# Two slot tiles of expert 0 inside the last tiles' routing of a GNN-plus-mixture-of-experts kernel

## The chip, the cores and the metric

The kernel runs on one core of one Trainium2 chip. The metric is the device time of an execution in microseconds (us). Before the change it is 1527.41 us, the median of three runs (1524.62 to 1529.33). One further execution was taken by the hardware profiler: its own time is 1522.34 us, of which 1520.5 us is the span from the first to the last instruction of the core. Durations below come from that execution. The engines are called PE (TensorE, matrix products; PEld is its weight load), DVE (VectorE), ACT (ScalarE), POOL (GpSimd) and SP (SyncE, which here only issues transfers).

## What is computed

1250 rows of 768 numbers pass a two-layer graph attention network and then one transformer block whose feed-forward part is a mixture of eight experts. The change touches only the end:

```python
x = x + _attention(_layernorm(x, ln1_g, ln1_b), Wqkv, Wproj)
x = x + _moe(_layernorm(x, ln2_g, ln2_b), Wrouter, W1, W2)
...
logits = xf @ Wrouter                          # 8 experts
topk_w, topk_idx = jax.lax.top_k(logits, 2)
topk_w = softmax(topk_w)
...
h = gelu(xf @ W1e)                             # 768 -> 384
acc = acc + we_e[:, None] * (h @ W2e)          # 384 -> 768
```

Only the two chosen experts of a token have a weight other than zero, so the kernel computes each expert for its own tokens alone.

## The kernel before

**Stages.** Ahead of the change stand the graph layers and the attention. Then comes a projection and routing stage over ten tiles of 125 tokens (`NT`, `T`), and last an expert stage. The two are the subject here.

**Projection and routing.** `product(t)` (L860) multiplies the attention's result with the projection weights (L864), adds the residual, takes the second layer norm into `yn` (one of three buffers of `RW` = 772 columns) and writes the sum `xs` to `out` (L875; even tiles are written from SP's queue, odd ones from ACT's). `route(t)` (L878) transposes `yn` (helper, L141), lets ACT apply the norm's scale and bias into `fT` (L147), forms the logits `pl` (L883), and DVE finds the best two experts. A product with a triangular matrix (`prk`, L900) and one with the tokens seen so far (L902, `seen`) give each token its rank within its expert. Rank plus 1280 times the expert is the slot. Columns 768 to 771 of `yn` take the token's number, its first expert and the two softmax weights; these use an Exp on ACT (L911). Two indirect transfers from POOL's queue (L923) then scatter the 125 rows into the DRAM buffer `xd`, one for each chosen expert. In the loop at L936 tile t+1's product is written ahead of tile t's route, and a scheduler interleaves them. `first_w`, the weights of expert 0, is loaded early in this stage (L854).

**Tiles beyond.** Every expert has three slot tiles of 128 rows (`CAP` = 384). After the last route, L943 to L951 count the slot tiles beyond that: one such tile (`EXTRA`) has a fixed job of its own, and any more are worked off by the conditional loop at L1032, whose number of passes (`more`) each engine loads into a register (L1031).

**Experts.** A job is an expert's three slot tiles, or the one extra tile. `fetch` (L967) loads slot rows from `xd` by SP (L970). `turn` (L991) transposes them on PE (L996) and lets ACT scale them (L997). `first` (L1001) is the first product with Gelu: 36 records on PE for each job (L1006). `second` (L1011) makes, for each slot tile, 12 records of the second product (L1015); DVE adds the weighted result to the row gathered from `out` (L1019; `results`, L986, is the gather on POOL), and POOL scatters it back (L1020). While job i runs its second product, job i+1's weights (L841, L842) and then its rows are loaded, and its rows are transposed between the second product's records. Loads, fetches and the register loads of `place` (L821, L822) all stand on SP's queue.

**What sets the order.** Tiles of a pool have a fixed number of buffers, and a transfer waits until the buffer it takes is free. Waits are set from what reads or writes the same tile or DRAM buffer; scatters into `xd` are declared independent of each other. The fetches of expert 0's rows (L1024) come after all scatters, and the conditional loop stands between that fetch and the first `turn` (L1046).

Of the kernel before, what the change touches and what calls it, by code (L numbers as in the profile page):

```python
# [10 lines left out]
F32 = mybir.dt.float32  # L11
F16 = mybir.dt.float16
BF16 = mybir.dt.bfloat16
I32 = mybir.dt.int32
# [13 lines left out]
def gnn_ffn_kernel(  # L28
# [27 lines left out]
    P = 128  # L56
# [22 lines left out]
    RW = D + 4  # L79
# [767 lines left out]

    with tc.tile_pool(name="proj", bufs=3, reuse_waits="tile") as pp, \
            tc.tile_pool(name="ppo", bufs=2, space=PSUM) as ppo, \
# [5 lines left out]

        normed = [pp.tile([P, RW], F32, tag=f"yn{i}", name=f"yn{i}", bufs=1) for i in range(3)]
# [3 lines left out]
        def product(t):  # L860
            po = ppo.tile([T, 2, 512], F32, tag="po", name="po")
            for s in range(2):
                for c in range(DC):
                    nc.tensor.matmul(po[:, s, :DH], aT[:, c, t * T:(t + 1) * T],  # L864
                                     wp[:, c, s * DH:(s + 1) * DH],
                                     start=(c == 0), stop=(c == DC - 1))
            y2 = pp.tile([T, D], F32, tag="y2", name="y2")
            ln_apply(y2, xs[:, t, :], st0[:, 0, t:t + 1], st0[:, 1, t:t + 1])
            o = y2.rearrange("p (s d) -> p s d", s=2)
            nc.vector.tensor_tensor(o, o, po[:, :, :DH], ALU.add)  # L870
            mean, rstd = ln_stats(y2)
            yn = normed[t % len(normed)]
            ln_apply(yn[:T, :D], y2, mean, rstd)
            nc.vector.tensor_add(xs[:, t, :], xs[:, t, :], y2)
            split_rows(nc.sync if t % 2 == 0 else nc.scalar, out[t * T:(t + 1) * T, :], xs[:, t, :])  # L875
            return yn

        def route(t, yn, seen):  # L878
            fT = pp.tile([P, DC, T], F32, tag="fT", name="fT", bufs=2)
            transpose_rows(ppt, yn[:T, :D], affine(fT, 0, 2))  # L880
            pl = ppl.tile([P, 512], F32, tag="pl", name="pl")
            for c in range(DC):
                nc.tensor.matmul(pl[:T, :NE], fT[:, c, :], wr[:, c, :],  # L883
                                 start=(c == 0), stop=(c == DC - 1))
            lg = small.tile([T, NE], F32, tag="lg", name="lg")
# [12 lines left out]
            nc.vector.tensor_add(both, oh[:, 0, :], oh[:, 1, :])  # L898
            pr = ppl.tile([P, 512], F32, tag="pl", name="prk")
# [8 lines left out]

            ex = small.tile([T, 2], F32, tag="ex", name="ex")
            nc.vector.tensor_sub(ex[:, 0:1], top[:, 1:2], top[:, 0:1])  # L910
            nc.scalar.activation(ex[:, 0:1], ex[:, 0:1], AF.Exp)  # L911
            nc.vector.tensor_scalar(ex[:, 1:2], ex[:, 0:1], 1.0, None, ALU.add)
            nc.vector.tensor_copy(yn[:T, D:D + 1], number[:, t:t + 1])
            nc.vector.tensor_copy(yn[:T, D + 1:D + 2], atf[:, 0:1])
            nc.vector.reciprocal(yn[:T, D + 2:D + 3], ex[:, 1:2])
            nc.vector.tensor_mul(yn[:T, D + 3:D + 4], ex[:, 0:1], yn[:T, D + 2:D + 3])
# [10 lines left out]
            return new  # L927
# [6 lines left out]
        yns = [product(0)]  # L934
        seen = None
        for t in range(NT):  # L936
            if t + 1 < NT:
                yns.append(product(t + 1))
            seen = route(t, yns[t], seen)


        pn = ppl.tile([P, 512], F32, tag="pl", name="pn")
        nc.tensor.matmul(pn[:, :NE], ones, seen, start=True, stop=True)  # L943
        count = small.tile([P, 1], F32, tag="count", name="count")
        nc.vector.scalar_tensor_tensor(used, pn[:, :NE, None].to_broadcast([P, NE, NR]), 0.0, used,
                                       op0=ALU.add, op1=ALU.is_gt, accum_out=count)
        nc.vector.tensor_scalar(more, count[0:1], -float(EXTRA), 0.0, ALU.add, ALU.max)
        nc.vector.tensor_tensor(used, used, beyond, ALU.mult)
        for i in range(EXTRA):
            pick(-1.0e9 if i == 0 else picked[:, i - 1, 1:2], i)  # L950
        nc.vector.tensor_copy(picked[:, EXTRA, :], picked[:, EXTRA - 1, :])  # L951
# [5 lines left out]
    with tc.tile_pool(name="moe", bufs=2, reuse_waits="tile") as mp, \  # L957
# [9 lines left out]
        def fetch(rows, n):  # L967
            xr = mp.tile([P, NS, RW], F32, tag="xr", name="xr")
            for s in range(n):
                nc.sync.dma_start(xr[:, s, :], rows[s * P:(s + 1) * P, :])  # L970
            return xr

        def tokens(xr, e, n, tag):

            ids = mp.tile([P, NS], I32, tag=tag + "ids", name="ids")
            nc.vector.tensor_copy(ids[:, :n], xr[:, :n, D])
            weight = mp.tile([P, NS], F32, tag=tag + "weight", name="weight")
            part = mp.tile([P, NS], F32, tag=tag + "part", name="part")
            nc.vector.tensor_sub(part[:, :n], xr[:, :n, D + 2], xr[:, :n, D + 3])
            nc.vector.scalar_tensor_tensor(part[:, :n], xr[:, :n, D + 1], e, part[:, :n],  # L980
                                           op0=ALU.is_equal, op1=ALU.mult)
            nc.vector.tensor_add(weight[:, :n], part[:, :n], xr[:, :n, D + 3])
            return ids, weight

        def results(ids, s, row):
            nc.gpsimd.indirect_dma_start(  # L986
                out=row, out_offset=None, in_=out,
                in_offset=bass.IndirectOffsetOnAxis(ap=ids[:, s:s + 1], axis=0),
                bounds_check=N - 1, oob_is_err=False)

        def turn(xr, n):  # L991
            xT = mp.tile([P, DC, CAP], F32, tag="xT", name="xT")
            for c in range(DC):
                pt = mpt.tile([P, 512], F32, tag="pt", name="pt")
                for s in range(n):
                    nc.tensor.transpose(pt[:, s * P:(s + 1) * P], xr[:, s, c * P:(c + 1) * P], ident)  # L996
                nc.scalar.activation(xT[:, c, :n * P], pt[:, :n * P], AF.Identity,  # L997
                                     scale=lnp[:, 2, c:c + 1], bias=lnp[:, 3, c:c + 1])
            return xT

        def first(w1, xT, n):  # L1001
            hT = mp.tile([P, FC, CAP], F32, tag="hT", name="hT")
            for f in range(FC):
                ph = mph.tile([P, 512], F32, tag="ph", name="phe")
                for c in range(DC):
                    nc.tensor.matmul(ph[:, :n * P], w1[:, c, f * P:(f + 1) * P], xT[:, c, :n * P],  # L1006
                                     start=(c == 0), stop=(c == DC - 1))
                nc.scalar.activation(hT[:, f, :n * P], ph[:, :n * P], AF.Gelu)
            return hT

        def second(w2, hT, s, ids, weight, row):  # L1011
            po = mpo.tile([P, 2, 512], F32, tag="po", name="poe")
            for d in range(2):
                for f in range(FC):
                    nc.tensor.matmul(po[:, d, :DH], hT[:, f, s * P:(s + 1) * P],  # L1015
                                     w2[:, f, d * DH:(d + 1) * DH],
                                     start=(f == 0), stop=(f == FC - 1))
            o = row.rearrange("p (s d) -> p s d", s=2)
            nc.vector.scalar_tensor_tensor(o, po[:, :, :DH], weight[:, s:s + 1], o, op0=ALU.mult, op1=ALU.add)  # L1019
            nc.gpsimd.indirect_dma_start(  # L1020
                out=out, out_offset=bass.IndirectOffsetOnAxis(ap=ids[:, s:s + 1], axis=0),
                in_=row, in_offset=None, bounds_check=N - 1, oob_is_err=False)

        xr = fetch(xd[0:CAP, :], NS)  # L1024
# [6 lines left out]
        over = nc.values_load(more[0:1, 0:1], min_val=0, max_val=NE * NR)  # L1031
        with tc.For_i(0, over, 1):  # L1032
# [5 lines left out]
            ids, weight = tokens(xo, picked[:, EXTRA, 0:1], 1, "o")  # L1038
            results(ids, 0, sofar[0])
            second(w2, first(w1, turn(xo, 1), 1), 0, ids, weight, sofar[0])  # L1040

        extra = [place(i) for i in range(EXTRA)]
        jobs = [(float(e), NS, expert(e), lambda e=e: xd[e * REG:e * REG + CAP, :]) for e in range(NE)]
        jobs += [(picked[:, i, 0:1], 1, chosen(e), lambda r=r: xd[ds(r, P), :])
                 for i, (e, r) in enumerate(extra)]
        xT = turn(xr, NS)  # L1046
        for i, (e, n, _, _) in enumerate(jobs):
            w1, w2 = w
            hT = first(w1, xT, n)
            ids, weight = tokens(xr, e, n, "")  # L1050
# [3 lines left out]
            if i + 1 < len(jobs):  # L1054
                _, m, ws, slots = jobs[i + 1]
                w = load_expert(mp.tile([P, 2 * DC * FF], F32, tag="w", name="we"), *ws)
                xr = fetch(slots(), m)
                xT = turn(xr, m)
            for s in range(n):
                second(w2, hT, s, ids, weight, rows[s])  # L1060
# [31 lines left out]
```

## Time and profile before

| What | us |
|---|---|
| Median of three runs | 1527.41 |
| Profiled execution, its own time | 1522.34 |
| Its span | 1520.5 |
| PE busy in the span | 1433.7 (94%) |
| DVE / ACT / POOL busy | 811.9 / 595.6 / 418.6 |
| Bytes moved | 124.66 MB, 82 GB/s on average |
| Tile 9's (the last tile's) scatters start on POOL | 1284.71 and 1285.99 |
| First fetch of expert 0's rows is issued | 1291.10 |
| First product of expert 1 starts | 1326.67 |
| Last scatter of results starts | 1513.17 |

The page gives the busy time of each engine, the span in 40 slices, the chain of work that ended last, and groups of instructions with what ended the idle time before them. A product in 32-bit floats appears as two records on PE. The operations of the change's stages in this execution:

| Operation | count, us of one |
|---|---|
| L864 product record, 384 columns | 240; 38 in a row take 12.45 |
| L1006 first-product records of one job, 384 columns | 36 take 11.61 |
| L1006 the same with 128 columns (the extra job) | 36 take 4.18 |
| L1015 second-product records of one slot tile | 12 take 3.87 |
| L997 eviction of transposed rows, 384 / 128 columns | 0.67 / 0.40 |
| L1019 weighted add on DVE | 1.02 |
| L923, L986, L1020 indirect transfer on POOL | 0.98 / 1.03 / 1.00 |
| Table load on ACT | 1.28 |
| `more` read into a register (L1031), by engine | 0.31 to 0.58 |

The granted clock of PE over the whole span is 0.963 of full speed.

### The profile page before, as it was taken

Reading aid. Unit: us, or ns where it says so; the run is one execution under the profiler, and the core shown is the slowest. Engines: PE = TensorE matmul, PEld = TensorE weight load, DVE = VectorE, ACT = ScalarE, POOL = GpSimd, SP = SyncE. Lnnn points to the kernel's source line nnn. Section 1 sums busy time; section 2 is a strip of 40 time slices with the busy share of each in tenths; the row PEclk is TensorE's granted clock in tenths of the full one; section 3 lists DMA queues with packets and bytes.
Section 4 is the critical chain, followed back from the end, with each engine's and each line's share of the span. In section 5 each row is a group of like instructions: output and inputs, shape, how many; then the busy total and the mean of one; then the engine's idle time right before and its main releaser. Section 6 shows DMA issues by size and latency. Waiting matters only on the chain.

```text
span 1520.5 us, 15858 instructions
## 1 busy us (share of the span) xinstructions
PE 1433.7 (94%) x5952; PEld 779.0 (51%) x5952; DVE 811.9 (53%) x1311; ACT 595.6 (39%) x924; POOL 418.6 (28%) x276
## 2 busy tenths in 40 slices
PE   6787999999999999999999999999989996899997
PEld 4574555556555555543343343344333664565654
DVE  6688456434036640127778778778787764111111
ACT  4221513205116521136556646646656354221211
POOL 5000000000000010006646646655657222122222
PEclk9758999999999999999999999999999997899999
DMA  7000020010021139920000000000120432855643
GB/s 207 22 2 11 11 73 0 0 32 1 15 88 45 57 100 396 407 86 0 22 1 0 22 1 21 1 22 0 28 75 1 144 119 107 300 172 185 219 153 134
DMA packets 48199, 124.66 MB, mean 82 GB/s; under 512 B 5629, under 2 KB 22207, under 8 KB 48120
## 3 DMA queue, kind: packets, MB, share of 16 engines
q1 hardware_dynamic: 31468, 57.36, 11.5%
q0 software_dynamic: 11968, 56.26, 9.8%
q10 hardware_dynamic: 4684, 9.99, 2.2%
q8 instruction: 48, 0.79, 0.2%
q14 instruction: 31, 0.25, 0.1%
HBM read 70.47 MB, written 57.60 MB: 84 GB/s over the span
## 4 chain that ended last, share of the span: by engine, by line
PE 67%; DVE 9%; issue 7%; ACT 4%; DMA 4%; POOL 1%; POOLq 0%; SPq 0%; ACTq 0%; DVEq 0%
PE pagg L524 13%; PE st L676 8%; PE ph L204 7%; PE pav L720 7%; PE pk L639 5%; PE pv L655 5%; PE phe L1006 5%; PE poe L1015 5%; PE pq L639 4%; DMA xd<-yn,slot 2%; DVE sT L706 2%; PE po L864 2%; ACT sT L679 1%; DVE most L685 1%; PE mb L701 1%
## 5 line engine op out<-in xcount | busy, mean ns | idle before, releaser
L712 POOL TENSOR_TENSOR acc<-acc,sT 125x834 f32<-125x834 f32 (+1 forms) x139 | 273.1, 1964 | 10.9
L524 PE MATMUL pagg<-h,wt 125*125 125x385 f32 (+1 forms) x800 | 263.5, 486 | 0.4 <-DVE wt L517 0.4
L685 DVE TENSOR_TENSOR most<-most,st 125x834 f32<-125x834 f32 (+1 forms) x144 | 147.0, 1021 | 105.5 <-ACT sT L679 102.6
L524 PEld LDWEIGHTS pagg<-h,wt 125*125 125x125 f32 x800 | 147.0, 187 | 104.7 <-DVE wt L517 3.5
L706 DVE TENSOR_TENSOR sT<-sT,mb 125x834 f32<-125x834 f32 (+1 forms) x180 | 174.1, 1015 | 22.6 <-PE mb L701 22.6
L707 ACT ACTIVATE sT<-sT 125x834 f32<-125x834 f32 (+1 forms) x180 | 158.4, 900 | 49.2 <-DVE sT L706 48.8
L679 ACT COPY sT<-st 125x834 f32<-125x834 f32 (+1 forms) x180 | 151.6, 848 | 52.4 <-PE st L676 50.7
L676 PE MATMUL st<-qk 64*125 64x417 f32 (+1 forms) x720 | 164.5, 556 | 3.9 <-DVE most L685 3.8
L720 PE MATMUL pav<-sT,v 125*64 125x417 f32 (+1 forms) x720 | 151.0, 532 | 9.0 <-ACT sT L707 9.0
L617 POOL MEMSET zero<- 128x772 f32 x1 | 0.7, 742 | 530.2 <-PE ptr L141 530.2
L712 POOL TENSOR_TENSOR acc<-sT 125x834 f32<-125x834 f32 (+1 forms) x18 | 35.4, 1965 | 274.6 <-ACT sT L707 274.6
L676 PEld LDWEIGHTS st<-qk 64*125 64x125 f32 x720 | 56.5, 184 | 99.1 <-issue 42.7
L720 PEld LDWEIGHTS pav<-sT,v 125*64 125x64 f32 x720 | 42.5, 136 | 105.7 <-issue 43.9
L1015 PE MATMUL poe<-we,hT 128*128 128x384 f32 x264 | 88.8, 486 | 0.0
L639 PE MATMUL pq<-yT,wqk 128*128 128x417 f32 (+1 forms) x216 | 88.1, 534 | 0.0
L864 PE MATMUL po<-wp,aT 128*125 128x384 f32 x240 | 87.5, 498 | 0.0
L1019 DVE SCALAR_TENSOR_TENSOR sofar<-poe,weight,sofar 128x768 f32<-128x768 f32 x25 | 25.4, 1018 | 114.6 <-PE poe L1015 107.7
L1006 PE MATMUL phe<-xT,we 128*128 128x384 f32 (+1 forms) x288 | 86.6, 460 | 0.0
L639 PE MATMUL pk<-yT,wqk 128*128 128x417 f32 (+1 forms) x216 | 84.0, 526 | 0.0
L204 PE MATMUL ph<-gw,xnT 128*125 128x384 f32 x240 | 81.4, 498 | 0.5 <-DMA gw<-in_L_gnn_W_dram 0.5
L655 PE MATMUL pv<-wv,yT 128*125 128x384 f32 x240 | 79.9, 490 | 1.4 <-issue 1.4
L528 DVE RECIPROCAL rz<-pagg 125x1 f32<-125x1 f32 x20 | 3.3, 166 | 141.5 <-PE pagg L524 141.5
(222 smaller groups left out, 1788.2 us busy)
## 6 DMA issues: line engine op xcount, KB each, us to landing
xd<-zero POOLq DMA_DIRECT2D x8, 3860.0 KB, 15.2
we<-in_L_ffn_W_dram SPq DMA_DIRECT2D x16, 1152.0 KB
xr<-xd SPq DMA_DIRECT2D x25, 386.0 KB
gw<-in_L_gnn_W_dram SPq DMA_DIRECT2D x2, 2304.0 KB
wqk<-in_L_ffn_Wqkv_dram SPq DMA_DIRECT2D x12, 384.0 KB
xres<-in_x_dram SPq DMA_DIRECT2D x10, 375.0 KB
xsd<-xres ACTq DMA_DIRECT2D x10, 375.0 KB
xn<-in_x_dram SPq DMA_DIRECT2D x9, 336.0 KB
```

The costliest lines, as they stand in the source:

```text
L204: nc.tensor.matmul(po[:, s, :DH], xT[:, c, t * T:(t + 1) * T], w[:, c, s * DH:(s + 1) * DH], start=(c == 0), stop=(c == DC - 1))
L524: nc.tensor.matmul(po[:, s, :DH + s], ws[j][:, (d - d0) * T:(d - d0 + 1) * T], h[:, j, s * DH:(s + 1) * DH + s], start=(j == 0), stop=(j = ...
L639: nc.tensor.matmul(pq[:, :w], wqk[:, c, i, :], yT[:, c, c0:c0 + w], start=(c == 0), stop=(c == DC - 1))
L676: nc.tensor.matmul(st[:T, i, :w], self.qk[r, 1, j * T:(j + 1) * T], self.qk[r, 0, self.c0:self.c0 + w], start=True, stop=True)
L679: nc.scalar.copy(s[:, :, :w], st[:T, :, :w])
L685: nc.vector.tensor_tensor(self.most[:, :, :w], prev[:, :, :w], st[:T, :, :w], ALU.max)
L706: nc.vector.tensor_tensor(s[:, :, :w], s[:, :, :w], self.mb[:T, :, :w], ALU.subtract)
L707: nc.scalar.activation(s[:, :, :w], s[:, :, :w], AF.Exp)
L712: nc.gpsimd.tensor_tensor(self.acc[:, :, :w], prev[:, :, :w], s[:, :, :w], ALU.add)
L720: nc.tensor.matmul(self.pav[r, :w], v[:, j, hd0:hd0 + HD], s[:, i, :w], start=(j == 0), stop=(j == NT - 1))
L1006: nc.tensor.matmul(ph[:, :n * P], w1[:, c, f * P:(f + 1) * P], xT[:, c, :n * P], start=(c == 0), stop=(c == DC - 1))
L1015: nc.tensor.matmul(po[:, d, :DH], hT[:, f, s * P:(s + 1) * P], w2[:, f, d * DH:(d + 1) * DH], start=(f == 0), stop=(f == FC - 1))
```

## The change

Four things are done.

1. **Routing without Exp.** `yn` has 771 columns: token number, first expert, and the difference of the two best logits. The weights are formed in the expert stage, by `tokens`, as 0.5 plus or minus half of tanh(difference / 2), where ACT computes the Tanh (pinned in program order after the Gelu). The token number is now written at the end of `product`.
2. **Two slot tiles of expert 0 within routing.** After tile 6's route, the count of expert 0's tokens is taken; if it is under 256, the running count is lifted so that later tokens get slots from 256 on. The first two slot tiles (256 rows) are then fetched on SP into `xr0`. The last three tiles' steps are written out by hand in PE's order: `go` advances `route` of tiles 7, 8, 9, `product` of tile 9 and `early`, a generator that transposes the two slot tiles, runs their first product with 256 columns, gathers the rows from `out`, and runs both second products with their adds and scatters into `out`. The two gathers stand on POOL ahead of tile 8's and tile 9's scatters.
3. **Tiles beyond counted earlier.** `tiles_beyond` stands ahead of `early`'s last third of the first product and of its second products.
4. **Slot rows ahead of weights.** Expert 0's job keeps its third slot tile only; that fetch is issued on SP ahead of the register load of `more`. In the job loop the next job's rows are fetched before its weights, in program order. The register loads of `place` stand behind the loop on SP, and four of the six `sofar` clears on POOL do too.

The new PE order, the loop and the job loop:

```diff
+        def early(w1, w2):
+            for xT in turn(xr0, SOON, sp, ppt, "tr"):
+                yield None
+            for hT in first(w1, xT, SOON, sp, ppl, "pl"):
+                yield None
+            ids, weight = tokens(xr0, 0.0, SOON, sp, "")
+            for s in range(SOON):
+                results(ids, s, soon[s])
+            for s in range(SOON):
+                second(w2, hT, s, ids, weight, soon[s], ppo)
+                yield None
...
+            if t == WITH - 1:
+                pn = ppl.tile([P, 512], F32, tag="pl", name="pfirst")
+                seen = tally[-1]
+                nc.tensor.matmul(pn[:, :NE], ones, seen, start=True, stop=True)
+                lift = small.tile([1, 1], F32, tag="lift", name="lift")
+                nc.vector.tensor_scalar(lift, pn[0:1, 0:1], -1.0, float(SOON * P), ALU.mult, ALU.add)
+                nc.vector.scalar_tensor_tensor(seen[0:1, 0:1], lift, 0.0, seen[0:1, 0:1], op0=ALU.max, op1=ALU.add)
+                xr0 = sp.tile([P, SOON, RW], F32, name="xr0")
+                for s in range(SOON):
+                    ins = nc.sync.dma_start(xr0[:, s, :], xd[s * P:(s + 1) * P, :])
...
+        with tc.manual_schedule(engines={mybir.EngineType.PE}):
+            a, b = route(NT - 3, yns[NT - 3], tally), product(NT - 1)
+            go(b, 3)
+            go(a)
+            go(b, 2)
+            go(a)
+            go(b, 4)
+            go(a, 2)
+            go(b, 3)
+            yns.append(go(b))
+            x = early(*w)
+            a, b = (route(t, yns[t], tally) for t in (NT - 2, NT - 1))
+            go(a)
+            go(x, DC)
+            go(a)
+            go(b)
+            go(x)
+            go(a, 2)
+            go(b)
+            go(x)
+            go(b, 2)
+            tiles_beyond(tally[-1])
+            go(x)
+            go(x, SOON)
...
-        xr = fetch(xd[0:CAP, :], NS)
+        xr, ins = fetch(xd[SOON * P:CAP, :], NS - SOON, pin)
...
-        over = nc.values_load(more[0:1, 0:1], min_val=0, max_val=NE * NR)
+        with tc.issue_after(ins.ins):
+            over = nc.values_load(more[0:1, 0:1], min_val=0, max_val=NE * NR)
+            extra = [place(i) for i in range(EXTRA)]
...
             if i + 1 < len(jobs):
                 _, m, ws, slots = jobs[i + 1]
+                xr, _ = fetch(slots(), m, pin)
                 w = load_expert(mp.tile([P, 2 * DC * FF], F32, tag="w", name="we"), *ws)
-                xr = fetch(slots(), m)
-                xT = turn(xr, m)
+                xT = last(turn(xr, m, mp, mpt, "pt"))
```

The weights of a slot row in `tokens`:

```diff
-            nc.vector.tensor_sub(part[:, :n], xr[:, :n, D + 2], xr[:, :n, D + 3])
-            nc.vector.scalar_tensor_tensor(part[:, :n], xr[:, :n, D + 1], e, part[:, :n],
-                                           op0=ALU.is_equal, op1=ALU.mult)
-            nc.vector.tensor_add(weight[:, :n], part[:, :n], xr[:, :n, D + 3])
+        pin(nc.scalar.activation(lead, xr[:, :n, D + 2], AF.Tanh, scale=0.5))
+        nc.vector.tensor_scalar(weight, xr[:, :n, D + 1], e, -0.5, ALU.is_equal, ALU.add)
+        nc.vector.tensor_mul(weight, weight, lead)
+        nc.vector.tensor_scalar(weight, weight, 0.5, None, ALU.add)
```

## The prediction

> **What bounds the kernel now.** I read the busy tenths of the page first. TensorE (PE) is at 9 of 10 nearly everywhere; its one late hole lies in slices 34 and 35, where its granted clock falls too.
>
> ```profile
> PE   6787999999999999999999999999989996899997
> ...
> PEclk9758999999999999999999999999999997899999
> ```
>
> The chain of work in order of time (start us, length, what) names the hole. The scatters of routed rows into `xd` end it, then the first fetch of slot rows, and dense products start only at 1302.
>
> ```profile
> 1262.47 27.77 DMA xd<-yn,slot x2
> 1291.10 0.37 SPq L970
> 1291.53 0.42 SPq L970
> 1292.00 5.05 DMA xr<-xd
> ...
> 1302.46 10.32 PE phe L1006 x32
> ...
> 1326.67 11.61 PE phe L1006 x36
> ```
>
> From 1326.67 (expert 1's first product) to the end, PE works without a gap in periods of 25.5 us (1326.67, 1352.18, 1377.68): 11.61 first product, 11.61 second, 2.3 transposes. So I measure the change by the moment at which expert 1's first product starts. The table of stretches (length; busy PE, PEld, DVE, ACT, POOL; granted clock; DMA share; GB/s) shows PE empty, then at half clock, then full:
>
> ```profile
> 1286.00:1291.00 5.00, 0.00 (x0) 0.00 (x0) 0.28 (x3) 0.00 (x0) 0.97 (x1) 0.50 0.42 163
> ...
> 1294.00:1298.00 4.00, 2.06 (x6) 0.87 (x6) 0.57 (x4) 0.40 (x1) 0.43 (x1) 0.50 0.97 313
> 1298.00:1302.00 4.00, 3.67 (x14) 2.57 (x15) 0.00 (x0) 2.32 (x5) 2.69 (x3) 0.62 1.04 399
> 1302.00:1306.00 4.00, 4.00 (x16) 2.54 (x16) 0.00 (x0) 2.87 (x4) 0.00 (x0) 1.00 1.03 408
> ```
>
> Last, the rows of the conditional loop (L1032). No pass of it runs, yet every engine leaves it through a row of waits, which end together at 1290.9 to 1291.5, and SP's list of waits (us in total, times, longest), the second fence, names what came last:
>
> ```profile
> L1032 SPq EVENT_SEMAPHORE  x16: 17/28/28, 1288.3 to 1290.9; - x16
> L1032 PEldq EVENT_SEMAPHORE  x13: 51/51/51, 1285.2 to 1291.4; - x13
> ```
>
> ```profile
> SPq L1032 <- DMA xd<-yn,slot: 1.5, 2, 1.0
> ```
>
> The skipped loop is therefore a barrier: each engine waits there for all work and transfers issued ahead of it. The last scatter starts on POOL at 1285.99, so the barrier costs 5.5 us from the start of the last indirect DMA to PE's release (1291.5). This decides the sum, because the change puts new work ahead of that barrier.
>
> **The change, part by part.** All times stand on before's clock.
>
> *Data.* Worked out from the reference's inputs, the first seven token tiles bring expert 0 269 tokens, which is over 256: the lift is zero and two slot tiles are full in time. Expert 0 has 369 in all (under 384); only expert 6 (419) goes beyond, by one tile. No pass of the loop runs, as before.
>
> *Exp removed from routing.* Two table loads of 1.28 us per tile leave ACT. PE is full there (10.16 us from prk to prk: 24 product records of 0.328 make 7.9, the rest routing), so tiles 0 to 5 gain nothing. But tile 6's scatter no longer waits for the Exp columns: POOL waited 10.93 us for L916 until 1261.18, while its slots were ready at 1256.36. It now starts near 1256.8, the second near 1258.1, and lands near 1262.3 (landings 3.0 to 3.4 us after the descriptors).
>
> *New fetch of two slot tiles* on SP, ahead of tile 8's output write there: issued near 1262.4, as that write becomes ready (1262.78), so it delays nothing. A fetch from issue to use took 3.3 us (1291.10 to 1294.39), the second row 1 us more: 1266.6. VectorE (DVE) waits for it (`ids`) in the middle of tile 7's routing, reaching it near 1266; PE needs that routing at 1267.9. Cover: about 1 us. Beyond that it costs one for one.
>
> *PE up to the early transposes.* From 1255.75: 36 product records x 0.328 = 11.8, two row transposes 1.3, tile 7's logits 1.1, ranks and count 0.8: 1270.8. The same work in before ended at 1270.7, so nothing is gained or lost here.
>
> *Twelve transposes.* They wait on two shared PSUM buffers, so ACT paces them: tile 8's evictions 2.2 (six x 0.365), two of 256 columns (between 0.40 at 128 and 0.67 at 384: 0.53), tile 9's root 0.3 and its two write issues 0.65, then four more. PE is through them at 1276.2. Tile 8's logits and tile 9's transposes stand behind: 1278.0.
>
> *First and second product of the two tiles.* 36 records at 256 columns lie between 4.18 us (128) and 11.61 (384): 7.9. Each third waits for a hand-off: tile 9's logits for the first Gelu (a table load 1.28 ahead of it: 1281.6), the tile-beyond count for the second Gelu, the last third for the rank read. With ranks 0.5 + 0.5, logits 1.1 and count 0.3 this ends at 1289.1; 24 records of the second product at 0.3225 = 7.7: 1296.9. The last routing slots come 2.2 us later than before (1286.6 against 1284.4), but no longer decide.
>
> *The clock, where a rule speaks against.* The Trainium skill, "TensorE: Matmul & The Clock Gate" (Part 1: The HAM clock gate), says that an idle window of about 3.4 us halves the clock and as much sustained work restores it. The row shows a longer stay: 0.50 from 1274 through 1298 over sparse work, full 4 us after dense work began. By the rule alone 3.4 us of the early work run at half speed, 1.7 lost; by the row perhaps all until the second product, 6 lost; by neither, 0. I take 1.7, since pieces of 2.6 us stand close together: second product done at 1298.6. The ends, 1296.9 and 1303, go into the range.
>
> *What then stands ahead of the barrier.* DVE adds the second tile (1.02), POOL starts its scatter 0.3 later, plus 5.5: PE is released 6.9 us after its second product, at 1305.5. Everything behind the barrier waits with it: the slot rows and weights of expert 1, and the remaining tile. The count of tiles beyond and the last slot tile's fetch (scatter landed near 1292.6, fetch 1296) are done by then; this is what the reordered count buys.
>
> *After the barrier.* The last job shows a one-tile job:
>
> ```profile
> 1503.66 4.18 PE L1006 MATMUL phe<-xT,we 128*128 128x128 f32 x36
> ...
> 1507.68 4.04 PE L1015 MATMUL poe<-we,hT 128*128 128x384 f32 x12
> ```
>
> Transposes paced by ACT (six x 0.40, with starts 2.9), then the rest of the first product: 6.0 us after the release. SP meanwhile loads two registers (0.77 and 0.48 with their checks: 1.8 us, now behind the barrier), issues three fetches (1.3) and expert 1's weights. Rows are there 7.3 us after release: PE stalls 1.3. Eighteen transposes of 384-wide rows paced by ACT (six x 0.67) with 12 product records between take 5.9: 13.2; with the clock 0.8: 14.0. Weights of 1.18 MB per half, queued behind 1.2 MB of rows at some 400 GB/s, land near 9 us. Rows ahead of weights thus matter only here, and W1 has 5 us to spare; in the steady 25.5 us periods either order is hidden.
>
> *Per job.* The added Tanh (0.2 as Exp took) stands between Gelu and the next eviction on ACT; PE may see 0.1 of it in seven jobs: 0.7. The removed DVE operations there, and 771 against 772 columns, I put at 0 (bounds -0.5 and +0.5), DVE being busy 4 us in 30.
>
> *Queues moved past.* POOL's two gathers (1.03 each) stand ahead of tile 8's scatters and wait for tile 9's output write, issued near 1274.4. With 3.3 to land they end at 1280.4; the scatters are due at 1281.7. If the write lands 4 us later, they slip into the barrier's slack of 9 us. The cleared `sofar` rows (0.8 each) now follow on POOL, two ahead of the barrier inside the 3.2 us of landing.
>
> *Sum.* Expert 1 starts at 1305.5 + 14.0 = 1319.5 instead of 1326.7: 7.2 gained; less 0.7 per-job cost: 6.5. Span 1520.5 - 6.5 = 1514.0; the profiled execution, 1522.34, becomes 1515.8. That execution lies 5.07 us under the median 1527.41, so on the median: 1520.9. About 17 us of PE work move into a hole, but ten go to the hand-offs, the second scatter's landing and a second start.
>
> **The rivals.**
>
> *Better overlap.* Clock stays full and hand-offs cost nothing: 1270.8 + 21.7 us of pure PE work = 1292.5, expert 1 at 1313, gain 13; time 1514. For it: ACT loses its table loads. Against: 0.50 in the same minutes before. Chance 0.15.
>
> *Given back in part.* Late rows, slower hand-offs or per-job costs of 0.5 leave 0 to 4 us: time near 1525. Chance 0.13.
>
> *Slower: the half clock lasts.* Place: the 15.6 us of first and second product before the barrier. Price: every microsecond of that work at half clock costs one more. 1.7 is in the sum; it decides from 8.2 us of the work at half speed (1.7 + 6.5). If all of it runs so, the second product ends near 1312.5 and expert 1 starts 7 us late: 1534. For it: clock 0.50 over sparse work from 1274. Against: full clock 4 us after dense work resumes. Chance 0.08.
>
> *Not what it says.* Other rounding of the logits could lift slots and make one loop pass: at least 6 us of weights plus 8.4 of PE with nothing beside, some 20 us slower: 1541. The counts exclude it by 13 and 15 tokens: 0.02.
>
> **How the numbers follow.** The forecast itself has 0.62, with its own range 1517 to 1525. About 0.3% (4.6 us) is what a measurement can tell from no change. Faster: 0.55 of the forecast's 0.62 and the 0.15; same: 0.07 and 0.13; slower: 0.10. The range 1514 to 1527 takes the forecast, most of the better overlap and most of the part given back.
>
> **What would show it.** In the profile after: early `phe` records between 1278 and 1290, early `poe` ending near 1299, a PE gap of about 7 us whose release is an `out_dram` scatter's landing, a 128-column `phe` group, then expert 1 near 1319. Wrong, if scatters of tile 9 release the barrier, if PE waits for the two-tile fetch, or if the 25.5 us period moves by more than 0.2.

## The result and the profile after

The changed kernel takes 1516.51 us (median of 14 runs, 1514.23 to 1521.76), the kernel before 1527.33 in the same series (1521.51 to 1530.67). The ratio of the two kernels' runs is 0.9938 (9.5 us), with a 95% interval from 0.9928 to 0.9949: on 1527 us that is 7.8 to 11.0 us gained. Forecast were 6.5 us and 1520.9; the time lies inside the range and below the forecast.

The profiled execution took 1518.66 us, its span 1516.8. The page's busy tenths and clock come first. The hole of slices 34 and 35 (6 and 8 tenths before) has shrunk to slice 35 (8), and the clock's dip there is shallower:

```profile
PE   6787999999999999999999999999988999899997
...
PEclk9758999999999999999999999999999998899999
```

TensorE's timeline (start us, length, engine, line, what; in brackets the idle time ahead of it and its releaser) shows the new work where the hole was:

```profile
1274.18 0.44 PE L856 MATMUL pt<-ident,xr 128*128 128x128 f32 x2 [0.98 <-ACT fT L149]
1275.22 0.89 PE L856 MATMUL pt<-ident,xr 128*128 128x128 f32 x4 [0.60 <-ACT fT L149]
...
1281.55 4.31 PE L867 MATMUL phe<-xT,first_w 128*128 128x256 f32 x12
...
1288.34 4.41 PE L867 MATMUL phe<-xT,first_w 128*128 128x256 f32 x12 [0.26 <-DVE lg L956]
...
1293.47 2.84 PE L867 MATMUL phe<-xT,first_w 128*128 128x256 f32 x12
1296.14 7.90 PE L900 MATMUL poe<-first_w,hT 128*128 128x384 f32 x24
```

Three equal thirds of the early first product take 4.31, 4.41 and 2.84 us: the same 12 instructions, at different clocks. The stretches of 1 us in which the clock changes show when (columns as in the prediction's table: the granted clock is the third number from the end):

```profile
1277.00:1278.00 1.00, 0.84 (x6) 0.60 (x6) 0.36 (x1) 0.92 (x3) 0.00 (x0) 0.93 0.78 249
...
1284.00:1285.00 1.00, 1.00 (x4) 0.79 (x4) 0.00 (x0) 0.72 (x1) 0.00 (x0) 0.66 0.64 252
...
1288.00:1289.00 1.00, 0.74 (x3) 0.57 (x3) 0.78 (x7) 0.00 (x0) 0.72 (x1) 0.55 0.49 197
...
1291.00:1292.00 1.00, 1.00 (x5) 0.80 (x4) 0.00 (x0) 0.00 (x0) 0.00 (x0) 0.74 0.08 16
```

Between the first two and between the last two the clock is 0.50. A mean of 0.93 in a microsecond is 0.14 us at half clock, so the half clock lasts 6.8 us (1277.9 to 1284.7) and again 3.4 us (1288.1 to 1291.5).

Behind the second product, which ends at 1304.04, the chain that ended last (start, length, what) shows the barrier. It begins with the landing of the last scatter of early results, then runs through the row of waits at the loop's exit:

```profile
1305.38 3.05 DMA out_dram<-soon,ids
1308.43 0.04 DVEq L1105
...
1309.39 0.05 DVEq L1105
1309.44 0.15 issue
1309.59 0.17 DVE ids L880
1309.76 0.48 PE pt L856
...
1323.83 11.61 PE phe L867 x36
```

TensorE stands still from 1304.04 to 1309.76, 5.7 us, and expert 1's first product starts at 1323.83. The loop's waits end together, as they did before:

```profile
L1105 SPq EVENT_SEMAPHORE  x16: 17/28/6382, 1299.3 to 1309.0; - x16
...
L1105 PEldq EVENT_SEMAPHORE  x13: 51/51/2013, 1304.1 to 1309.4; - x13
```

The two first profiles differ by only 3.7 us, the medians by 10.8. Profiles of different executions can't be set side by side from zero: the start varies. So from here on every profile is cut at two moments, the first matmul of the projection (`po`, for which nothing ahead was changed) and the first matmul of expert 1. The table holds all profiles of this study, in us; "second product" is the end of expert 0's early one, counted from the first `po`.

| profile | first `po` at | second product | TensorE resumes | expert 1 | from there to the end | first `po` to end |
|---|---|---|---|---|---|---|
| before | 1160.86 | | 133.5 | 165.65 | 193.99 | 359.64 |
| before, again | 1164.27 | | 134.3 | 167.58 | 193.95 | 361.53 |
| after | 1162.74 | 141.30 | 147.01 | 160.93 | 193.13 | 354.06 |
| after, again | 1160.26 | 141.28 | 147.12 | 160.98 | 192.96 | 353.94 |
| after, third | 1160.08 | 138.07 | 143.80 | 158.10 | 193.12 | 351.22 |
| after, loop last | 1162.85 | 142.16 | 143.27 | 155.35 | 197.30 | 352.65 |
| after, transposes thrice | 1163.14 | 137.71 | 143.75 | 158.09 | 192.97 | 351.06 |
| after, late count | 1160.46 | 137.85 | 143.91 | 158.18 | 193.16 | 351.34 |
| after, order altered | 1164.78 | 135.09 | 141.48 | 155.35 | 193.07 | 348.42 |
| after, order altered and loop last | 1164.92 | 135.17 | 136.27 | 148.36 | 197.12 | 345.48 |
| before, loop last | 1159.78 | | 131.52 | 165.02 | 196.70 | 361.72 |
| before, Tanh alone | 1162.04 | | 134.65 | 168.39 | 193.37 | 361.76 |
| before, rows first alone | 1168.24 | | 133.92 | 169.08 | 193.88 | 362.96 |

By this cut the two profiles of before average 360.6 and the three of after 353.1: 7.5 us gained, singly between 5.6 and 10.3. Of this 6.6 lie ahead of expert 1 and 0.9 behind. The 6.6 can be followed in the table: from TensorE's resuming to expert 1, before needs 32.1 and 33.3 us, after 13.9, 13.9 and 14.3, as two thirds of expert 0 are done by then. That is 18.7 us less, and TensorE resumes 12.1 us later.

### The profile page after: what moved, and what is told of

It is laid out like the page before. It is cut to its first block, busy times and chain, and to the rows that moved or that the text cites. A ratio compares the mean times of both kernels' runs of the same rounds, so it can differ in the third digit from the quotient of the medians.

```text
span 1516.8 us, 15936 instructions
## 1 busy us (share of the span) xinstructions
PE 1437.4 (95%) x5990; PEld 784.6 (52%) x5990; DVE 808.4 (53%) x1287; ACT 574.4 (38%) x915; POOL 418.4 (28%) x278
## 3 DMA queue, kind: packets, MB, share of 16 engines
q1 hardware_dynamic: 31468, 57.35, 11.6%
q0 software_dynamic: 11968, 56.21, 10.2%
## 5 line engine op out<-in xcount | busy, mean ns | idle before, releaser
L206 PE MATMUL ph<-gw,x1T 128*125 128x384 f32 x240 | 79.2, 491 | 0.0
```

The costliest lines, as they stand in the source:

```text
L206: nc.tensor.matmul(po[:, s, :DH], xT[:, c, t * T:(t + 1) * T], w[:, c, s * DH:(s + 1) * DH], start=(c == 0), stop=(c == DC - 1))
```

## The experiments

**Theory and rivals.** The theory is that the gain is TensorE work moved into its hole, and that what remains to be lost there is the skipped loop's barrier and the half clock. There are three rivals: a side edit (Tanh, rows first, the early count) carries the gain; the barrier is only the place where a late transfer shows; the clock falls whatever the change does. The ratios below are to the kernel before, run in the same series.

### 1. The loop behind the last job

The changed kernel; the block moves as it is:

```
-        with tc.For_i(0, over, 1):
...
         for i, (e, n, _, _) in enumerate(jobs):
...
+        with tc.For_i(0, over, 1):
```

> The changed kernel with the conditional loop over tiles beyond moved behind the last expert job (its loop count is zero here, so no work moves with it). Theory: in the changed kernel nothing that TensorE needs is late when it meets the loop; what it waits for there, 5.7 us, is the loop's own barrier, which holds every engine until the scatters of the soon rows have landed. Without it TensorE goes from the second products of expert 0 (end 1304.0) straight to the transposes of tile 2, whose rows were fetched at 1298.2. Expected: 1516.5 - 5.7 = 1510.8 us, down to 1508 if the clock then stays up through tile 2's first products. Rival: the wait is for tile 2's rows or for an engine behind, and the loop only shows it; then 1515 to 1517 us and the same idle time under another name.

Measured: 1513.61 us (4 runs), ratio to before 0.9905 (0.9873 to 0.9936), where 1510.8 was expected. The interval overlaps that of the changed kernel, so the profile has to speak. TensorE's timeline:

```profile
1297.11 7.90 PE L900 MATMUL poe<-first_w,hT 128*128 128x384 f32 x24
1306.12 0.44 PE L856 MATMUL pt<-ident,xr 128*128 128x128 f32 x2 [1.11 <-DVE ids L880]
...
1308.39 3.88 PE L867 MATMUL phe<-xT,first_w 128*128 128x128 f32 x32
...
1318.20 11.78 PE L867 MATMUL phe<-xT,we 128*128 128x384 f32 x36
```

The hole of 5.7 us is 1.1, and the releaser named for that is VectorE, which takes tile 2's `ids` right behind its last add of early results: the wait was the barrier's own. The clock stays at 1.00 from 1293 on, so 12.1 us lie between resuming and expert 1 in place of 13.9. Against the two profiles of after whose first two thirds were also slow, expert 1 is 5.6 us earlier, as expected. But the end is not: the stretch behind it grows by 4.2 us (193.1 to 197.3). The moved loop's exit stands in the tail (the loop's waits; last column: first and last start):

```profile
L1125 SPq EVENT_SEMAPHORE  x16: 17/28/3217, 1471.7 to 1508.8; - x16
...
L1125 POOLq EVENT_SEMAPHORE  x13: 17/43/342, 1506.0 to 1509.0; - x13
```

The last scatter starts at 1505.68, the loop's waits end at 1509.1, and only then come the program's closing steps: 9.8 us from that scatter to the end, against 7.3 in after (1509.48 to 1516.8). That is 2.5 of the 4.2. The remaining 1.7 arise ahead of it: the last job's gather starts 4.9 us after the scatter that it waits for (1495.98 to 1500.91), against 3.2 in after; the cause of this is open. A barrier moved to the end is not free, a point that neither side of this expectation had.

### 2. The same move in the kernel before

> The kernel before with its conditional loop moved behind the last expert job, and nothing else. Theory: TensorE's hole of 10.3 us stays, because expert 0's slot rows can be fetched only when the last scatter has landed; the changed kernel's fetch came 3.07 us after its last scatter's start, the kernel before's came 5.1 us after it, so 2.0 us are the barrier's: 1527.3 - 2.0 = 1525.3 us. Rival: the change won mainly by taking the register loads and the barrier out of the wait, not by giving TensorE work in it; then this edit alone brings 5 us or more (1522 or less).

Measured: 1526.82 us (12 runs), 0.9996 (0.9983 to 1.001): no difference. The end of the hole in the kernel before, then this run's timeline:

```profile
1294.39 0.69 PE L996 MATMUL pt<-ident,xr 128*128 128x128 f32 x2 [10.29 <-DMA xr<-xd]
```

```profile
1282.45 0.58 PE L943 MATMUL pn<-seen,ones 125*128 125x8 f32 x2
1291.30 0.66 PE L996 MATMUL pt<-ident,xr 128*128 128x128 f32 x2 [8.28 <-DMA xr<-xd]
```

The hole is 8.3 us where before's was 10.3: the 2.0 expected, and what remains is the wait for expert 0's rows. Expert 1 starts 0.6 us earlier than in the first profile of before and 2.6 earlier than in the second; how long the half clock goes on behind the hole makes the difference (9.0 us here, 6.6 and 8.8 there). The tail pays 2.7. Moving the barrier alone brings nothing; work in the hole was needed.

### 3. TensorE's order altered

```
-            go(b, 3)
+            x = early(*w)
+            a = route(NT - 2, yns[NT - 2], tally)
+            for _ in range(3):
+                go(x, 2)
+                go(b)
             yns.append(go(b))
-            x = early(*w)
-            a, b = (route(t, yns[t], tally) for t in (NT - 2, NT - 1))
+            b = route(NT - 1, yns[NT - 1], tally)
             go(a)
-            go(x, DC)
+            go(x)
...
```

The early transposes now stand between the last products. After them come: tile 8's transposes, a third of the first product, tile 8's logits, a third, tile 9's transposes, tile 8's ranks, tile 9's logits, the last third, tile 9's ranks, the count, the second products.

> The changed kernel with TensorE's hand-written order altered: the transposes of the two early slot tiles stand two by two between the last products of the projection's last tile, and the routing of tile 8 and 9 stands between the thirds of the first product. Theory: the half clock of 1278 to 1294 comes of thin work with gaps from 1272 to 1278 (transposes waiting for ScalarE); the thirds of the first product then take 2.6 to 2.8 us instead of 4.3 and 4.4, and the second products end some 4 us earlier, although tile 9's routing begins 2.6 us later: 1516.5 - 4 = 1512.5 us. Rival: the clock drops anyway when TensorE passes from dense projection work to mixed work, or tile 9's later routing takes back what is won: 1515 to 1519 us.

Measured: 1514.31 us (4 runs), 0.992 (0.989 to 0.995). The timeline:

```profile
1274.85 0.61 PE L856 MATMUL pt<-ident,xr 128*128 128x128 f32 x4
...
1276.72 2.76 PE L867 MATMUL phe<-xT,first_w 128*128 128x256 f32 x12
...
1280.95 2.86 PE L867 MATMUL phe<-xT,first_w 128*128 128x256 f32 x12 [0.26 <-DVE lg L956]
...
1286.70 4.46 PE L867 MATMUL phe<-xT,first_w 128*128 128x256 f32 x12
...
1306.26 0.69 PE L856 MATMUL pt<-ident,xr 128*128 128x128 f32 x2 [6.40 <-DVE weight L885]
```

Two thirds run at full clock; the third meets a dip that came later (1287.8 to 1291.2), after the many short instructions of 1283 to 1287. There was no gap ahead of this dip: TensorE was busy in every microsecond from 1281 to 1288. The second products end at 135.1, and expert 1 starts at 155.35 against a mean of 160.0 in after: 4.6 us by the profile, 2.2 by the medians, with overlapping intervals. The barrier costs a little more here (6.4 us from the second product to resuming, in after 5.7 to 5.8).

### 4. Both together

> Both: TensorE's order altered as in the run with the altered order, and the conditional loop behind the last expert job. Theory: the second products end about 1300, and tile 2's rows (fetched some 3.1 us after the last scatter's start, landing some 2 us later) are there at 1300 to 1302, so the two savings add up to all but 1 or 2 us: 1516.5 - 5.7 - 4 + 1.5 = 1508 us, perhaps 1506. Rival: with the barrier gone the last tile's scatters set the time, and the altered order, which starts tile 9's routing later, brings nothing on top of the moved loop: 1511 us or more.

Measured: 1511.01 us (4 runs, 1507.08 to 1512.22), 0.9888 (0.9857 to 0.9919). The interval lies below that of the changed kernel, and every run below all sixteen runs of the changed kernel (the lowest is 1513.15). The timeline:

```profile
1292.10 7.99 PE L900 MATMUL poe<-first_w,hT 128*128 128x384 f32 x24
1301.19 0.44 PE L856 MATMUL pt<-ident,xr 128*128 128x128 f32 x2 [1.11 <-DVE ids L880]
...
1313.28 11.77 PE L867 MATMUL phe<-xT,we 128*128 128x384 f32 x36
```

The time is 3 us above the 1508 expected and just what the rival named (1511 or more). But the rival's mechanism, late scatters, falls, since TensorE waits 1.1 us and no more: expert 1 starts at 148.36, 11.6 us ahead of after's mean, so ahead of it the savings add up. What is missing is the 4 us that the tail pays for the moved loop, as in run 1. First `po` to end is 345.5 against 353.1. This version beats both kernels.

### 5. Early transposes issued three times

```
-            for s in range(n):
+            for s in [s for s in range(n) for _ in range(again)]:
...
-            for xT in turn(xr0, SOON, sp, ppt, "tr"):
+            for xT in turn(xr0, SOON, sp, ppt, "tr", 3):
```

> The changed kernel with each of the twelve early transposes issued three times over (the same rows into the same place, so the result is the same): 24 more short TensorE instructions in the gaps where it waits for ScalarE. Theory: the early first product ran at half clock because TensorE stood still in four gaps of 2.2 us in all just ahead of it; filled, its thirds fall from 4.3 and 4.4 us toward the 2.8 that the run with the altered order showed, and the second products end 2 to 3 us before 1304.0, at most 3.5: 1513.5 to 1514.5 us. Rival: the clock follows something else (the width or the kind of the work, other engines' load); then 24 added transposes cost 2 to 5 us of TensorE's time ahead of tile 9's routing and the time is 1517 to 1521 us.

Measured: 1515.71 us (4 runs), 0.9929 (0.9904 to 0.9954), which doesn't separate from after. The profile does separate them:

```profile
1277.31 2.40 PE L856 MATMUL pt<-ident,xr 128*128 128x128 f32 x18 [0.18 <-ACT xT L857]
...
1281.46 2.76 PE L867 MATMUL phe<-xT,first_w 128*128 128x256 f32 x12
...
1286.70 2.86 PE L867 MATMUL phe<-xT,first_w 128*128 128x256 f32 x12 [0.26 <-DVE lg L956]
...
1290.27 2.84 PE L867 MATMUL phe<-xT,first_w 128*128 128x256 f32 x12
1292.95 7.90 PE L900 MATMUL poe<-first_w,hT 128*128 128x384 f32 x24
```

All thirds run at full clock (1.00 in every microsecond from 1272 to 1296). The product's kind and width are unchanged, so they are not the cause; thin work ahead of it is. (This rests on one profile, against five with the same order and no filling, each of which shows half clock there.) The added transposes cost 1.3 to 1.5 us themselves, so that the second products end at 137.7: 3.6 earlier than in after's first two profiles, but only 0.4 earlier than in its third.

### 6. The count of tiles beyond put back

```
-            tiles_beyond(tally[-1])
             go(x)
             go(x, SOON)
+            tiles_beyond(tally[-1])
```

> The changed kernel with the count of tiles beyond put back behind the second products of the two early tiles (that part of the change undone alone). Theory: the barrier is released by the landing of the last soon scatter (1308.4), while the count's chain on VectorE takes 1.9 us and would end near 1307, so it stays hidden: 1516.5 us, within 0.5. Rival, as the prediction had it: counting ahead of the second products buys time; then the chain stands behind the last product and the release comes 2 us later: 1518.5 us.

Measured: 1518.44 us (7 runs, 1510.96 to 1521.24), 0.9945 (0.9922 to 0.9967). The timeline:

```profile
1290.41 7.90 PE L900 MATMUL poe<-first_w,hT 128*128 128x384 f32 x24
1298.15 0.29 PE L1021 MATMUL pn<-seen,ones 125*128 125x8 f32 x2
1304.37 0.69 PE L856 MATMUL pt<-ident,xr 128*128 128x128 f32 x2 [5.94 <-DVE ids L880]
```

From the second products' end (1298.31) to TensorE's resuming are 6.1 us, in after 5.7 to 5.8: 0.2 to 0.4 us more. But the second products end 0.2 us earlier than in after's third profile, as the two `pn` instructions no longer stand ahead of them, so TensorE resumes only 0.1 us later (143.91 against 143.80). The chain is hidden under the scatter's landing, as the theory here had it and not the prediction. The median, 1.9 above after's, can't be told from it by the intervals; the profile shows nothing of the rival's 2 us.

### 7. Tanh alone, in the kernel before

```
-            nc.scalar.activation(ex[:, 0:1], ex[:, 0:1], AF.Exp)
...
+            pin(nc.scalar.activation(lead[:, :n], xr[:, :n, D + 2], AF.Tanh, scale=0.5))
```

> The kernel before with the routing weights taken from a Tanh in the expert jobs instead of an Exp in the routing (that part of the change alone; slot rows one column narrower). Theory: in the full stretches TensorE hides it; only in tile 9's tail, where ScalarE's table loads stood in the chain (TensorE waited 1.33 us for the Exp columns there), 1.5 to 2.5 us go, and the period of the expert jobs, 25.5 us before and 25.36 after, shows whether this edit makes it shorter: 1525 us. Rival, as the prediction had it: the tail gains nothing and the jobs lose 0.1 us each: 1528 us. Second rival: it brings 4 us and more, so that it and not the early tiles carries much of the gain: 1523 us or less.

Measured: 1525.6 us (20 runs), 0.9996 (0.9984 to 1.0008): nothing. Tile 9's tail in the kernel before, then the same in this run and the period of its jobs:

```profile
1276.94 1.51 PE L141 MATMUL ptr<-ident,yn 125*128 125x125 f32 x6 [1.33 <-DVE ex L912]
```

```profile
1278.20 1.51 PE L141 MATMUL ptr<-ident,yn 125*128 125x125 f32 x6 [1.06 <-DVE yn L134]
...
1330.43 11.77 PE L1001 MATMUL phe<-xT,we 128*128 128x384 f32 x36
...
1355.79 11.77 PE L1001 MATMUL phe<-xT,we 128*128 128x384 f32 x36
```

The wait for the Exp columns (1.33 us) has become one for the layer norm (1.06): behind the stall removed stood the next one, only 0.27 us shorter. My expectation of 1.5 to 2.5 there was wrong. The period is 25.36 us, that of after, against 25.50 before. In the timeline the Tanh shifts the interleaving: three pairs of second-product instructions stand between the transposes, before two, and cover more of their wait for ScalarE. Six such periods lie behind expert 1's start, which would make 0.8 us; the stretch to the end is 0.6 us shorter (193.37 against 193.97).

### 8. Rows ahead of weights alone, in the kernel before

```
-                w = load_expert(mp.tile([P, 2 * DC * FF], F32, tag="w", name="we"), *ws)
-                xr = fetch(slots(), m)
+                xr = fetch(slots(), m, pin)
+                w = load_expert(mp.tile([P, 2 * DC * FF], F32, tag="w", name="we"), *ws)
```

> The kernel before with the next expert's slot rows fetched ahead of its weights (that part of the change alone). Theory: in the periods of 25.5 us both are there long before they are needed, and expert 1's rows only come sooner while its weights come later, so the time stays: 1527.3 us, within 1. Rival: this edit makes the period 25.36 us and gives expert 1 an earlier start, 1 to 3 us in all: 1525 us.

Measured: 1524.1 us (12 runs), 0.9993 (0.9978 to 1.0007): nothing, as expected; the stretch behind expert 1's start is 193.88. The start itself, at 169.1, is the latest of all, with waits for rows of expert 0 in the hole, whose fetch this edit doesn't touch. The profiled execution (1533.03 us) was the slowest of the twelve.

### 9. Both kernels again

> The changed kernel unaltered, for a second profile. Theory: what differs from profile to profile of one kernel is first the input loads in the first 25 us (up to 5 us, nothing to do with the change), and second how long the half clock lasts over the early first product. Counted from the projection's first product to expert 1's first product, the first profile of the changed kernel took 160.9 us, and the run with the late count, with the same TensorE order up to there, 158.2: I expect a value between the two, and 193.0 to 193.2 us from there to the end. Rival: 160.9 is what the changed kernel takes, and the late count really is 2.7 us faster: 160.5 to 161.3.

> As the run before it, a third profile of the changed kernel: the same expectation, a value from 158 to 161 us between the two first products, not the same one in all three profiles.

> The kernel before unaltered, for a second profile. Theory: from the projection's first product to expert 1's first product it takes 165.65 us in the first profile and does so again within 0.5, since TensorE is idle where the clock falls and waits for transfers; from there to the end 194.0 us. The start of the projection may differ by some us. Rival: this stretch varies here as much as in the changed kernel (2 us and more).

Measured: 1516.09, 1513.15 and 1527.66 us, one execution each. After gave 160.98, which alone would have fitted the rival, and then 158.10, which doesn't: the spread is the kernel's own, and 158.2 of the late count is near one of its two values. The third profile of after, its thirds and then its clock:

```profile
1277.91 3.61 PE L867 MATMUL phe<-xT,first_w 128*128 128x256 f32 x12
...
1284.00 2.86 PE L867 MATMUL phe<-xT,first_w 128*128 128x256 f32 x12 [0.26 <-DVE lg L956]
...
1287.58 2.84 PE L867 MATMUL phe<-xT,first_w 128*128 128x256 f32 x12
```

```profile
1276.00:1277.00 1.00, 1.00 (x8) 1.00 (x8) 0.17 (x1) 0.00 (x0) 0.00 (x0) 0.61 0.00 0
...
1279.00:1280.00 1.00, 1.00 (x4) 0.80 (x4) 0.00 (x0) 0.98 (x4) 0.60 (x1) 0.68 0.86 233
```

Here the half clock lasts 3.4 us (1276.2 to 1279.6), where the first profile has 6.8 and 3.4. Before gave 167.58, so its stretch varies by 1.9, more than the 0.5 expected. The start of all varies too. In the second profile of before TensorE waits 4.17 us for the first weights,

```profile
23.07 7.36 PE L204 MATMUL ph<-gw,xnT 128*125 128x384 f32 x15 [4.17 <-DMA gw<-in_L_gnn_W_dram]
```

and 0.51 in the first: it is 3.8 us behind at 23 us and 3.4 at the first `po`. Both of the first two profiles (before and after) had an early start.

## Why the prediction was right, and where not

The mechanism was right: work moved ahead of the barrier, a release by an `out_dram` scatter's landing, a two-tile and a one-tile part. By its steps, on the clock of the first `po` (1160.86 in the profile that the prediction used):

- *PE up to the early transposes, twelve transposes.* Forecast through at 1276.2, which is 115.3; measured 1278.1, which is 115.4. Tiles 0 to 5 gained nothing, as forecast: from the first `po` to tile 6's ranks 94.8 us against 94.5.
- *First and second product.* Forecast without clock loss 136.0. Taking half of the half-clock time off the measured ends gives 141.3 - 5.1 = 136.2 and 138.1 - 1.7 = 136.4: right. TensorE waited nowhere for the two-tile fetch.
- *The clock.* Forecast 1.7 us lost, by the rule in the Trainium skill, "TensorE: Matmul & The Clock Gate" (Part 1: The HAM clock gate): windows of about 3.4 us. Measured is 1.7 in one profile of after and 5.1 in two. The pieces measured, 3.4, 3.4 and 6.8 us, do fit one, one and two such windows; but I counted one of them, and two profiles had three. This term was mis-sized, by up to 3.4 us, and it is the largest source of spread in the changed kernel. Nor was the window ahead of a fall idle, as the rule has it: in the first profile TensorE was busy for 64% and 87% of the 3.4 us ahead of its two falls, in run 3 for all of it, mostly with short instructions.
- *What then stands ahead of the barrier.* Forecast 6.9 us from the second product to the release, measured 5.7 to 5.8 in after: 1.1 too much. I added the whole 5.5 of before's barrier; here 3.05 of landing and 1.3 to TensorE's start are what follows the scatter's start at 1305.38. The step also says that the fetch of tile 2 and the count are done by then: true, but what "the reordered count buys" is only 0.1 us by TensorE's resuming (run 6).
- *After the barrier.* Forecast 14.0, measured 13.9, 13.9 and 14.3, but here luck had a part. The first product of tile 2 ended 7.8 us after the release in the first profile (1309.75 to 1317.57), not 6.0, most of it at half clock, and the stall of 1.3 us for expert 1's rows did not come. The clock cost more than the 0.8 set for it: run 1, at full clock, needs 1.8 less. Rows ahead of weights mattered nowhere that a run could show.
- *Per job.* Forecast 0.7 lost, measured 0.9 gained in all. The sign was wrong: I costed the Tanh as time between two evictions, and the interleaving that came with it was better by 0.14 us in each job (run 7).
- *The sum.* Expert 1 was forecast at 158.6; the three profiles give 160.93, 160.98 and 158.10. Set against the one profile of before that the sum was made for (165.65), 7.2 was forecast and 5.6 is the mean. But that profile was early in this stretch too: its repetition took 167.58. The whole gain by the profiles, 7.5 against 6.5 forecast, is a sum of errors that partly cancel: on average the clock took 2.3 us more than forecast, while the release gave 1.1 more, the jobs 1.6, and the mean of before lies 1.0 later than the one profile used.
- *The barrier itself* was seen, but its removal not thought of: moved to the end, with the order altered, it brought 7.6 us by the profile on top of the change's 7.5 (run 4).

Of the rivals, the half clock was the right one to fear: it took 5.1 us in two profiles of three, not the 8.2 from which it decides. Better overlap (expert 1 at 1313, 152.1) was reached only by run 4's version.

What stays open: the runs differ by 9.5 us (by the ratio), the profiles by 7.5 on average. With two and three profiles, each moving by 2 to 3 us, that is no contradiction, but no run shows where the other 2 us are. That the early tiles carry the gain rests on the trace (18.7 us less to do behind the hole) and on exclusion: Tanh and rows first alone show no gain, and by their intervals can bring at most 2.4 and 3.4 us, the count 0.1 to 0.4. The early tiles alone were not run; neither were the moved register loads and clears, nor Tanh together with the early tiles, where an earlier scatter of tile 6 could help.

## What to carry to other kernels

A loop that makes no pass can still be a barrier: before moving work ahead of one, ask what that work adds to what it waits for, and whether the loop could stand elsewhere. Price the half clock by how long the work around it stays thin, window by window, and fill or reorder the gaps ahead of dense work. Cut every profile at a moment that the change can't touch, and take more than one profile before explaining a few microseconds.

## What the runs showed that was not expected

- Useless transposes in four gaps of 2.2 us in all kept TensorE's clock at 1.00 over 24 us (one profile), where the same kernel without them had 3.4 to 10.2 us of half clock (three profiles).
- A skipped loop costs at the end too: 2.5 us between the last scatter and the end of the program (9.8 against 7.3), 2.8 in the kernel before (10.2 against 7.3).
- The landing of the first weights moves the whole program: the first product on them starts between 18.7 and 24.4 us in the thirteen profiles, a spread of 5.7 us in a stage that no edit touches.
